# Sending attention scores through memory instead of through TensorE, in a two-layer graph network

## The chip, the cores and the metric

The kernel runs on one core of a Trainium2 chip. The metric is the device time of one execution in microseconds; several executions are timed and their median is taken. A profile of one execution gives, for each engine, when every instruction began and how long it took. The engines are TensorE (PE, with its weight loads shown as PEld), VectorE (DVE), ScalarE (ACT), GpSimd (POOL) and SyncE (SP), which here does nothing but issue DMAs.

## The reference, cut to what matters

There are 128 graphs of 64 nodes, each node a row of 768 numbers. Layer 0 mixes neighbours with three weight matrices and is not touched by the change, except in how it writes its last result to memory. Layer 1 is graph attention with 6 heads of 128 columns:

```python
h = jnp.einsum('bni,hio->bhno', feat_in, W)
th = jnp.tanh(h)
attn_src = jnp.einsum('bhno,hoz->bhnz', th, w_src)
attn_dst = jnp.einsum('bhno,hoz->bhnz', th, w_dst)
attn = attn_src + jnp.swapaxes(attn_dst, -1, -2)
attn = jnp.where(attn >= 0, attn, leaky_alpha * attn)
attn = jnp.where(mask, NEG_MASK, attn)
attn = jax.nn.softmax(attn, axis=-1)
feat_out = jnp.einsum('bhnm,bhmo->bhno', attn, h) + b
gate = jax.nn.sigmoid(feat_in @ H_w.T + H_b)
out = gate * feat_out + (1.0 - gate) * feat_in
```

So each node n has one source score and one destination score per head. The logit of the pair (n, m) is source score of n plus destination score of m. A node's own score lies on the partition of that node, and can be added there as a bias. The other node's score has to appear along the free axis, for all 64 nodes of the graph, on every partition: a turn and a spread. How that is done is what changes.

## The kernel before, in words

The 8192 rows are 64 tiles of 128 rows (two graphs each), worked on as 32 pairs of tiles. Pass 1 (layer 0) runs over all pairs, then pass 2 (layer 1) runs over all pairs. All five engines have an order of instructions written out by hand, SP too.

In pass 1, `finish` closes each pair: `dev` and `norm` make the layer norm of the result on ScalarE (`HF`), `turn` transposes its 32x32 blocks on VectorE into `HT` (L862), `put_turned` (called tput in the lists) stores `HT` to `H1D` in one DMA per tile (L865), and `half_of` makes `HH_` on ScalarE (L852). `HF`, `HT` and `HH_` share three buffers, so the second `HH_` of a pair waits until the first tile's `HT` has been stored. In pass 2, `load_h` reads `H1D` back as the operand of the products, with the blocks put into their right places by the read: four DMAs of 96 KB per tile, in pieces of 32 numbers (L372).

Pass 2 runs a list of step names, `ORDER`, once per pair. A name such as `cp1/2` means step `cp`, tile 1, of the pair that is two behind. `Pk.q` is a half product on TensorE: 30 per pair, each two 512-column instructions in the trace (L1121). `att` is the weighing of the rows (L1286). `R` and `RA` add products into `hz` on VectorE and ScalarE, `Ff` forms operands on VectorE. Each engine follows the list in its own instructions only, and runs ahead until something it needs isn't there. `END` is the list for the last pairs.

The path of the scores, tile by tile: `th` (tanh, ACT), `mul` (both products with the score weights, DVE, L1163), `sum` (sums by head, ACT, L1173), `k` and `chain` (POOL: separate the two graphs, L1176, and split the scores into three bf16 parts, L1184 and L1186), `rows` (PE, L1206: turn them), `rrow` (DVE, L1210) and `lrow` (ACT, L1215) take the result out of PSUM, `log` (PE, L1225: one product gives source plus destination for all heads), `cp` (DVE, L1229: take the logits where there is an edge, over a tile that `memset` filled), `pre` (ACT, L1234: leaky ReLU), `tr` (DVE, L1238: largest), `exp` (ACT, L1246). Then `tv` turns the blocks of the exponentials on DVE, `ts` stores them with four DMAs (L1272), `tl` loads them back (L1278), `swap` loads the other graph's rows (L1192), and `att` follows.

Pass 1 already has a small case of the form that the change brings to the scores: `turn_degrees` transposes a 128x32 tile on DVE (L603), `put_degrees` stores it (L606), and `get_degrees` reads it back with two loads that repeat a row over 64 partitions (L612).

Of the kernel before, what the change touches and what calls it, by code (L numbers as in the profile page):

```python
# [15 lines left out]
P = 128  # L16
# [81 lines left out]
dma0/4 R1/1 RA1/1 P3.1/1 R2/1 memset1/2 R14/2 th1/2 R3/1 tv1/3 P11.0/1 rows0/2 P4.0/1 rrow0/2  # L98
lrow0/2 tl0/3 mul1/2 P6.0/1 Ff1 P4.1/1 R4/1 Ff6/1 log0/2 P6.1/1 P11.1/1 sum1.2/2 R6/1 sum1.3/2
sum1.0/2 Ff7 sum1.1/2 P7.0/1 k1/2 cp0/2 Ff4 lx1/3 P7.1/1 rec0/3 Ff2 P9.0/1 Ff8 Ff11/1 R7/1 P9.1/1  # L100
pre0/2 RA7/1 tr0/2 chain1/2 P8.0/1 Ff9 P8.1/1 R9/1 lx0/3 rows1/2 Ff10 memset0/1 ld R11/1 g1/3
exp0.0/2 ts1/3 rrow1/2 R8/1 P10.0/1 P10.1/1 exp0.1/2 Ff3 swap0/3 lrow1/2 th0/1 P12.0/1 tv0/2 R10/1
P12.1/1 mul0/1 tl1/3 g0/2 att/3 log1/2 R12/1 ev1.0/3 ev1.1/3 cp1/2 sum0.3/1 ev0.0/3 sum0.1/1 P13.0/1
e1/3 f1.0/3 P13.1/1 P14.0/1 sum0.0/1 P14.1/1 P2.0 P2.1 R13/1 ev0.1/3 P1.0 pre1/2 f1.1/3 sum0.2/1
tr1/2 f1.2/3 P0.0 P0.1 e0/3 dma1/3 P5.0 f0.0/3 swap1/2 P5.1 exp1.0/2 RA0 R0 P1.1 exp1.1/2 f0.1/3
ts0/2 RA5 k0/1 chain0/1 rec1/2 Ff5 RA14/1 P3.0 f0.2/3 R5 RA2
# [4 lines left out]
FINISH = (158, 189, 215, 216, 242, 268)  # L111
# [4 lines left out]
P3.1/2 P11.0/2 RA1/2 Ff6/2 swap0/4 R2/2 R1/2 P4.0/2 R14/3 Ff1/1 rows0/3 Ff11/2 tv1/4 P4.1/2 Ff4/1  # L116
memset1/3 R3/2 rrow0/3 g0/3 tl0/4 th1/3 P8.0/2 lrow0/3 Ff2/1 P6.0/2 R4/2 P6.1/2 Ff3/1 log0/3 P7.0/2
P8.1/2 mul1/3 cp0/3 R6/2 pre0/3 sum1.2/3 ts1/4 Ff8/1 P7.1/2 Ff7/1 R7/2 tr0/3 rec0/4 RA7/2 Ff9/1
P9.0/2 P9.1/2 P11.1/2 tl1/4 Ff5/1 sum1.0/3 R9/2 R8/2 sum1.1/3 P10.0/2 R11/2 P10.1/2 sum1.3/3 th0/2
Ff6/1 Ff10/1 R10/2 att/4 P13.0/2 lx0/4 mul0/2 dma0/5 exp0.0/3 g1/3 ev1.0/4 g0/2 ev0.1/4 ev1.1/4  # L120
ev0.0/4 sum0.2/2 k1/3 g1/4 P13.1/2 P0.0/1 chain1/3 P12.0/2 P5.0/1 memset1/2 rows1/3 R13/2 rrow1/3
P2.0/1 e1/4 P1.0/1 e0/4 lx1/4 f1.0/4 f0.0/4 P12.1/2 f1.1/4 sum0.0/2 P2.1/1 lrow1/3 R12/2 ld/1 P5.1/1
log1/3 P0.1/1 f0.1/4 f1.2/4 exp0.1/3 sum0.3/2 P14.0/2 f0.2/4 R5/1 P14.1/2 sum0.1/2 RA0/1 P1.1/1 R0/1
P3.0/1 k0/2 cp1/3 RA2/1 R14/2 RA1/1 Ff11/1 R1/1 P3.1/1 RA14/2 tv0/3 pre1/3 chain0/2 tr1/3 lx0/3 R2/1
th1/2 rows0/2 mul1/2 P4.0/1 P8.0/1 lrow0/2 exp1.0/3 R3/1 rrow0/2 exp1.1/3 P8.1/1 tv1/3 P4.1/1 Ff1
sum1.2/2 memset0/2 lx1/3 R4/1 RA5/1 Ff2 Ff4 sum1.0/2 sum1.1/2 log0/2 Ff7 P6.0/1 P6.1/1 R6/1 Ff3
cp0/2 swap1/3 sum1.3/2 P7.0/1 k1/2 P7.1/1 P9.0/1 RA7/1 P9.1/1 R8/1 swap0/3 chain1/2 Ff8 pre0/2
rows1/2 ts0/3 P11.0/1 ts1/3 tr0/2 P11.1/1 tl1/3 lrow1/2 rec1/3 Ff9 exp0.0/2 rec0/3 R7/1 P10.0/1
exp0.1/2 rrow1/2 R9/1 Ff10 R11/1 dma0/4 log1/2 tv0/2 cp1/2 P10.1/1 R10/1 tl0/3 P12.0/1 P12.1/1 att/3
dma1/4 th0/1 pre1/2 P13.0/1 mul0/1 tr1/2 g0/1 R12/1 g1/2 sum0.0/1 sum0.1/1 P14.0/1 ev0.1/3 ev1.1/3  # L130
ev1.0/3 ev0.0/3 sum0.3/1 k0/1 sum0.2/1 e1/3 P13.1/1 e0/3 swap1/2 R13/1 f1.0/3 PH0 P14.1/1 swap0/2
f0.0/3 f1.1/3 RA14/1 PH2 exp1.0/2 R14/1 chain0/1 PH1 f1.2/3 PH5 exp1.1/2 RAH0 tv1/2 memset0/1 f0.1/3
rows0/1 f0.2/3 lrow0/1 th1/1 ts0/2 mul1/1 PH3 RAH5 PH11 RAH2 tl0/2 RAH1 PG0 RH3 PH4 Ff5 RH4 PH6 Ff6
dma0/3 sum1.0/1 PH7 sum1.2/1 rrow0/1 sum1.1/1 RH6 rec0/2 RAH7 log0/1 PH9 dma1/3 Ff11 lx0/2 cp0/1
sum1.3/1 k1/1 PH8 RG0 RH9 RH11 PH10 pre0/1 RH8 PH12 chain1/1 rows1/1 tr0/1 ts1/2 th0 RH10 lx1/2
rec1/2 tl1/2 mul0 memset1/1 rrow1/1 att/2 exp0.0/1 exp0.1/1 sum0.1 lrow1/1 PH13 PG3 tv0/1 ev0.1/2
RH13 ev0.0/2 log1/1 RH12 sum0.2 ev1.0/2 sum0.0 sum0.3 cp1/1 ev1.1/2 e0/2 pre1/1 lx0/1 PH14 swap0/1
f0.0/2 g1/1 ts0/1 tr1/1 PG2 RAH14 f0.1/2 RG2 k0 f0.2/2 chain0 e1/2 PG1 RG1 PG8 RG3 f1.0/2 PG4
exp1.0/1 PG5 exp1.1/1 dma0/2 rows0 th1 tv1/1 lrow0 swap0 RG4 f1.1/2 PG6 mul1 memset0 tl0/1 f1.2/2
sum1.1 RG6 rrow0 att0/1 rec0/1 PG7 PG9 log0 RG7 PG10 sum1.0 RG5 dma1/2 sum1.2 ev0.0/1 sum1.3 PG11  # L140
cp0 ts1/1 swap1/1 ev0.1/1 k1 pre0 tl1/1 RG9 chain1 tr0 e0/1 rows1 rec1/1 RG11 lrow1 f0.0/1 att1/1
exp0.0 lx0 rrow1 exp0.1 log1 f0.1/1 ev1.0/1 ev1.1/1 RG8 memset1 cp1 e1/1 turnp0 lx1/1 RG10 PG12 pT0
f1.0/1 rec0 pre1 f1.1/1 f1.2/1 att0 tr1 RG12 g0 PG14 exp1.0 ev0.0 PG13 ev0.1 e0.0 swap1 exp1.1 lx1
turnp1 dma1/1 f0.0.0 e0.1 f0.2/1 f0.1.0 f0.0.1 f0.2.0 RG13 f0.3.0 f0.1.1 rec1 out0.0 RG14 f0.2.1 pT1
att1 ev1.1 e1.1 ev1.0 g1 f1.0.1 dma0/1 e1.0 f0.3.1 f1.1.1 f1.0.0 out0.1 f1.2.1 f1.1.0 f1.3.1 f1.2.0
f1.3.0 out1.1 out1.0
# [4 lines left out]
def kernel(  # L151
# [82 lines left out]
    Q = 32  # L234
    NQ = P // Q


    H0D = [dram.tile([KB * P, P], F32, name=f"h0_{t}") for t in range(NT)]
    CTD = [dram.tile([4 * P, P], BF16, name=f"ct_{p}") for p in range(NP)]
# [127 lines left out]
    def load_h(p):  # L367
        for k in range(2):
            t = 2 * p + k
            H1[t] = keep.tile([P, D], F32, name="h1", tag="x", bufs=6)  # L370
            for f in range(NQ):
                nc.sync.dma_start(  # L372
                    H1[t][f * Q : (f + 1) * Q].rearrange("i (b n) -> i b n", n=Q),
                    H1D[p][k].rearrange("(b i) (f n) -> f i b n", i=Q, n=Q)[f])

    def fetch():


        def load_block(n):
            j, q = int(n[1]), int(n[2])  # L380
            to = bw2[n].rearrange("p (k s n) -> p k s n", k=KQ, s=2)
            for s, src in enumerate((w_cat, hw_t)):
                nc.sync.dma_start(
                    to[:, :, s, :],
                    src.rearrange("(j k p) n -> j p k n", k=KQ, p=P)[j][:, :, q * CQ : (q + 1) * CQ])

        return ([(62, lambda: load_h(0)), (67, lambda: nc.sync.dma_start(hbb, row(hb, P)))]
                + [(i, lambda n=n: load_block(n)) for i, n in (
                    (7, "b10"), (13, "b00"), (13, "b21"), (25, "b11"), (31, "b01"), (37, "b20"),
                    (49, "b22"), (49, "b02"), (61, "b12"))]  # L390
                + [(i, lambda n=n: sum_of_weights(bw2, n)) for i, n in (
                    (22, "g10"), (28, "g6"), (41, "g12"), (46, "u"), (50, "g14"), (57, "w"),
                    (59, "g5"), (65, "v"), (67, "g3"), (70, "g9"), (73, "g1"), (76, "g8"),
                    (79, "g11"))])


    with ExitStack() as px:
# [441 lines left out]
        def finish(p, k):  # L839
# [24 lines left out]
            def put_turned():  # L864
                nc.sync.dma_start(H1D[p][k].rearrange("(b p) n -> p b n", p=P),  # L865
                                  HT[t].rearrange("p (b n) -> p b n", b=KB))
# [174 lines left out]
    with ExitStack() as px:  # L1041
# [7 lines left out]
        def load(p):  # L1049
            if p >= NP:  # L1050
                return
            if p:
                load_h(p)
            AI[p] = work.tile([P, 2, N], I32, name="ai", bufs=4)
            nc.sync.dma_start(
                AI[p], adj[p * 2 * GT : (p + 1) * 2 * GT].rearrange("(t g) i j -> (g i) t j", g=GT))
# [22 lines left out]
        for g in range(GT):  # L1079
            nc.gpsimd.memset(gm[g * N : (g + 1) * N, g : g + 1], 1.0)  # L1080
        lrow, rrow, sdb = [], [], []
# [73 lines left out]
        TH, PR, SD, SG, PS, AM, AL, PB, DN, MX, PT, PO, FF, EE, HX, TP = ({} for _ in range(16))  # L1155
# [5 lines left out]
        def multiply(t):  # L1161
# [3 lines left out]
            SD[t] = small.tile([P, 2, H], F32, name="sd")  # L1165
            SG[t] = small.tile([P, 3, H], F32, name="sg")

        def sums(t, i):

            j = 1 - i // 2  # L1170
            for h in range(i % 2 * HH, (i % 2 + 1) * HH):
                to = SD[t][:, 1, h : h + 1] if j else SG[t][:, 2, h : h + 1]
                nc.scalar.activation(PR[t][:, j, h, :], PR[t][:, j, h, :], AF.Copy, accum_out=to)  # L1173

# [42 lines left out]
        def fill(t):  # L1217
            AM[t] = work.tile([P, H, N], F32, name="a")
            nc.gpsimd.memset(AM[t], NEG_MASK / LEAKY)
# [12 lines left out]
        def leaky(t):  # L1232
            al = AL[t] = work.tile([P, H, N], F32, name="al", bufs=1)
            nc.scalar.activation(al, AM[t], AF.Prelu, alpha=LEAKY)  # L1234
# [5 lines left out]
        def exps(t, i):  # L1240

            if i == 0:
                PB[t] = work.tile([P, H, N], F32, name="pb")
# [103 lines left out]
        def store(t):  # L1347
# [6 lines left out]
            "rec": one_over, "tv": turn_blocks, "ts": put_blocks, "tl": get_blocks, "turnp": turn_p, "pT": copy_p,  # L1354
# [5 lines left out]
        def step(n, p):  # L1360
            if n == "att":
                attend_both(p)
            elif n == "ld":
                load(p + 1)
            elif n[0] == "F":
# [158 lines left out]
```

## Time and profile before

| | |
|---|---|
| median of 3 runs | 2336.75 us (2336.64 to 2336.89) |
| profiled execution, its own time | 2335.71 us |
| its span | 2333.9 us |
| PE busy | 2308.5 us, 99% of the span |
| DVE busy | 1952.9 us, 84% |
| ACT busy | 1280.4 us, 55% |
| POOL busy | 442.2 us, 19% |
| mean granted TensorE clock | 0.997 |

The span is what the profiled engines cover; the execution's own time is 1.81 us longer. Pass 2 takes about the last 900 us of the span. Busy times in the profile add up overlapped instructions once, but the mean duration of one instruction includes the overlap with the next: the distance from one start to the next is what an engine really pays. In timelines the columns are start, duration, engine, line and operation.

### The profile page before, as it was taken

The numbers are of one execution on the slowest core, as the hardware profiler recorded it, in microseconds if no ns is written. First come the engines' busy times: TensorE is split into PE (matmuls) and PEld (weight loads), VectorE is DVE, ScalarE is ACT, GpSimd is POOL, SyncE is SP. The second block draws the span as 40 slices with busy tenths as digits, with TensorE's granted clock in tenths as the row PEclk, the third lists the DMA queues.
The fourth block names the chain that finished last, engine by engine and source line by source line (L and its number), as shares of the span: only waits on it lengthen the run. The fifth ranks groups of instructions, "written<-read, shape, count | busy, mean of one in ns | idle before, by whom it ended". The sixth has DMA issues, their size and how long they took to land.

```text
span 2333.9 us, 35510 instructions
## 1 busy us (share of the span) xinstructions
PE 2308.5 (99%) x11441; PEld 1645.1 (70%) x11441; DVE 1952.9 (84%) x3738; ACT 1280.4 (55%) x3843; POOL 442.2 (19%) x1097
## 2 busy tenths in 40 slices
PE   9999999999999999999999999999999999999996
PEld 7888888888888888888888885444444444444445
DVE  8877777777777777777777777899999999999999
ACT  3454454454454543543544523677776667776776
POOL 1111111111111111111111101122222222222222
PEclk9999999999999999999999999999999999999998
DMA  5335535535445446445445367667677777776667
GB/s 190 91 98 130 136 100 134 129 100 144 119 104 148 112 107 157 105 110 155 100 114 152 98 164 148 122 139 147 139 144 152 150 146 141 145 146 138 141 134 164
DMA packets 805127, 308.89 MB, mean 132 GB/s; under 512 B 622676, under 2 KB 755143, under 8 KB 804940
## 3 DMA queue, kind: packets, MB, share of 16 engines
q1 hardware_dynamic: 795868, 282.20, 50.6%
q0 software_dynamic: 8928, 24.38, 6.0%
q8 instruction: 90, 1.47, 0.3%
q14 instruction: 97, 0.79, 0.1%
q10 hardware_dynamic: 144, 0.04, 0.0%
HBM read 140.11 MB, written 140.87 MB: 120 GB/s over the span
## 4 chain that ended last, share of the span: by engine, by line
PE 95%; DVE 3%; DMA 2%; issue 0%; SPq 0%; ACT 0%; DVEq 0%; ACTq 0%
PE pwa L814 21%; PE pwb L814 18%; PE pwcd L814 14%; PE pma L1121 14%; PE pmb L1121 11%; PE pmd L1121 5%; PE pmc L1121 5%; PE pb L742 3%; PE ps L1286 1%; PE pwcd L798 1%; PE pwcd L742 1%; PE ps L1225 1%; DMA weights<-in_wself_t_dram 1%; DMA weights<-in_wadj_t_dram 1%; PE pmc L1286 0%
## 5 line engine op out<-in xcount | busy, mean ns | idle before, releaser
L814 PE MATMUL pwa<-weights,op 128*128 128x256 f32 x2304 | 529.6, 379 | 0.3 <-DVE x L806 0.3
L814 PEld LDWEIGHTS pwa<-weights,op 128*128 128x128 f32 x2304 | 427.5, 190 | 56.0 <-issue 1.1
L814 PE MATMUL pwb<-weights,op 128*128 128x256 f32 x1932 | 451.3, 381 | 0.0
L814 PEld LDWEIGHTS pwb<-weights,op 128*128 128x128 f32 x1932 | 361.9, 190 | 51.4 <-issue 0.8
L347 DVE TENSOR_TENSOR op<-op 128x768 f32<-128x768 f32 x310 | 290.2, 945 | 94.5 <-ACT op L752 91.6
L814 PE MATMUL pwcd<-weights,op 128*128 128x256 f32 x1560 | 357.8, 379 | 0.0
L814 PEld LDWEIGHTS pwcd<-weights,op 128*128 128x128 f32 x1560 | 296.1, 190 | 40.1
L1121 PE MATMUL pma<-weights,op_f 128*128 128x512 f32 x620 | 291.5, 592 | 0.0
L1173 ACT ACTIVATE pr<-pr 128x128 f32<-128x128 f32 x768 | 225.5, 295 | 89.0 <-DVE pr L1163 89.0
L752 ACT COPY op<-pb 128x512 f32<-128x512 f32 (+1 forms) x132 | 70.8, 617 | 357.0 <-PE pb L742 357.0
L1121 PEld LDWEIGHTS pma<-weights,op_f 128*128 128x128 f32 x620 | 117.7, 190 | 147.8 <-issue 138.4
L324 POOL TENSOR_SCALAR rn<-su 128x1 f32<-128x1 f32 x124 | 25.0, 202 | 846.8 <-ACT hf L319 528.5
L1121 PE MATMUL pmb<-weights,op_f 128*128 128x512 f32 x372 | 181.0, 594 | 0.0
L547 ACT ACTIVATE hp<-x,rn 128x768 f32<-128x768 f32 x60 | 109.2, 1820 | 108.6 <-POOL rn L326 108.6
L1173 ACT ACTIVATION_READ_ACCUMULATOR pr<-pr 128x1 f32 x768 | 143.5, 187 | 0.0
L318 ACT ACTIVATE hf<-x 128x768 f32<-128x768 f32 x64 | 53.6, 837 | 148.9 <-DVE x L850 148.8
L1246 ACT ACTIVATE pb<-al,mx 128x64 f32<-128x64 f32 x384 | 128.1, 337 | 12.6 <-DVE mx L1238 12.4
L1348 POOL DMA_DIRECT2D out_dram<-f x62 | 55.1, 898 | 390.4 <-DVE f L1345 372.0
L1121 PEld LDWEIGHTS pmb<-weights,op_f 128*128 128x128 f32 x372 | 68.4, 190 | 84.0 <-issue 76.3
L1121 PE MATMUL pmb<-weights,h 128*128 128x512 f32 x248 | 122.8, 596 | 0.0
L806 DVE TENSOR_TENSOR x<-pwcd,x 128x256 f32<-128x256 f32 x127 | 53.3, 420 | 81.7 <-PE pwcd L798 81.5
L1121 PE MATMUL pmc<-weights,op_f 128*128 128x512 f32 x248 | 121.6, 592 | 0.0
(240 smaller groups left out, 4121.0 us busy)
## 6 DMA issues: line engine op xcount, KB each, us to landing
x<-in_x_dram SPq DMA_DIRECT2D x64, 384.0 KB
h<-ht SPq DMA_DIRECT2D x64, 384.0 KB
out_dram<-x SPq DMA_DIRECT2D x64, 384.0 KB
hh<-hh SPq DMA_DIRECT2D x64, 384.0 KB
h<-h SPq DMA_DIRECT2D x256, 96.0 KB
x<-hh SPq DMA_DIRECT2D x64, 384.0 KB
out_dram<-f POOLq DMA_DIRECT2D x62, 384.0 KB, 6.2
h<-hpt SPq DMA_DIRECT2D x60, 384.0 KB
```

The costliest lines, as they stand in the source:

```text
L318: nc.scalar.activation(by, src, AF.Copy, scale=-1.0 / D, accum_out=sums[:, 0:1])
L324: nc.gpsimd.tensor_scalar(to[:, 0:1], sums[:, 1:2], 1.0 / D, EPS, op0=OP.mult, op1=OP.add)
L347: return (nc.vector.tensor_add if s1 == "+" else nc.vector.tensor_sub)(to, x, y)
L547: nc.scalar.activation(hp.rearrange("p (b f i) -> p b f i", b=KB, f=NQ), X[t].rearrange("p (b i f) -> p b f i", b=KB, f=NQ), AF.Relu, scal ...
L742: nc.tensor.matmul(to[:, g, :, i, :], H0[2 * p + k][o, kb * P : (kb + 1) * P], rts[p % 2][o, k, :n].rearrange("p s n -> p (s n)"), start=T ...
L752: nc.scalar.copy(a[:, :n].rearrange("p s h (g n) -> p g (s h) n", g=GT), ps[:, :, c * n * KQ * N : (c + 1) * n * KQ * N].rearrange("p g (x ...
L806: nc.vector.tensor_add(v, bank[b][:, :CQ], v)
L814: nc.tensor.matmul(bank[b][:, :CQ], OPS[p, an][:, s, q, :], bw[bn][:, (s * KQ + q) * CQ : (s * KQ + q + 1) * CQ], start=(first and q == s ...
L1121: nc.tensor.matmul(bank[p, b], operand(p, an)[:, q, :], bw2[bn][:, 2 * q * CQ : 2 * (q + 1) * CQ], start=(first and q == 0), stop=(q == KQ ...
L1173: nc.scalar.activation(PR[t][:, j, h, :], PR[t][:, j, h, :], AF.Copy, accum_out=to)
L1246: nc.scalar.activation(PB[t][:, h, :], AL[t][:, h, :], AF.Exp, bias=MX[t][:, h : h + 1], accum_out=DN[t][:, h : h + 1])
L1348: nc.gpsimd.dma_start(of[t * P : (t + 1) * P, :], FF[t], accum_op=OP.add)
```

## The change

For all pairs but the last two (`BY_PE = 2`), the two products on TensorE and what serves them (`k`, `chain`, `rows`, `rrow`, `lrow`, `log`, `pre`) are gone. The sums of the destination scores go into a 128x32 tile `sdt`, which VectorE transposes (`sv`); one DMA stores it to memory (`ss`), two DMAs read it back with every head's 64 scores repeated over the 64 partitions of the graph (`sl`); ScalarE then does, for each head, the leaky ReLU of that plus the source score as a bias (`lk`), and VectorE chooses by edge from SBUF (`cl`). The other edit moves the reordering of `H1D`: `put_turned` now stores with four DMAs in pieces of 32 numbers, and `load_h` reads each tile with one DMA. `le` loads the second tile of a pair at its own place. `ORDER`, `END` and `FINISH` are new lists.

```diff
+    BY_PE = 2
+    SDD = [dram.tile([P, Q], F32, name=f"sd_{t}") for t in range(NT)]
...
-    def load_h(p):
-        for k in range(2):
+    def load_h(p, *ks):
+        for k in ks:
             t = 2 * p + k
             H1[t] = keep.tile([P, D], F32, name="h1", tag="x", bufs=6)
-            for f in range(NQ):
-                nc.sync.dma_start(
-                    H1[t][f * Q : (f + 1) * Q].rearrange("i (b n) -> i b n", n=Q),
-                    H1D[p][k].rearrange("(b i) (f n) -> f i b n", i=Q, n=Q)[f])
+            nc.sync.dma_start(H1[t].rearrange("p (b n) -> p b n", b=KB),
+                              H1D[p][k].rearrange("(b p) n -> p b n", p=P))
...
             def put_turned():
-                nc.sync.dma_start(H1D[p][k].rearrange("(b p) n -> p b n", p=P),
-                                  HT[t].rearrange("p (b n) -> p b n", b=KB))
+                for f in range(NQ):
+                    nc.sync.dma_start(
+                        H1D[p][k].rearrange("(b i) (f n) -> f i b n", i=Q, n=Q)[f],
+                        HT[t][f * Q : (f + 1) * Q].rearrange("i (b n) -> i b n", n=Q))
...
-            SD[t] = small.tile([P, 2, H], F32, name="sd")
+            SD[t] = sdt[t % 2] if t // 2 < NP - BY_PE else small.tile([P, 2, H], F32, name="sd")
...
+        def turn_scores(t):
+            ST[t] = work.tile([P, Q], F32, name="st2")
+            nc.vector.transpose(ST[t], SD[t])
+
+        def put_scores(t):
+            nc.sync.dma_start(SDD[t], ST[t])
+
+        def get_scores(t):
+            DR[t] = work.tile([P, GT, H, Q], F32, name="dr")
+            for g in range(GT):
+                at = SDD[t][g * N : g * N + H, :]
+                nc.sync.dma_start(
+                    DR[t][g * N : (g + 1) * N].rearrange("p f h n -> p f (h n)"),
+                    bass.AP(tensor=at.tensor, offset=at.offset,
+                            ap=[[0, N], [Q * Q, N // Q], [1, H * Q]]))
+
+        def leaky_sum(t):
+            PB[t] = work.tile([P, H, N], F32, name="pb")
+            for h in range(H):
+                nc.scalar.activation(PB[t][:, h, :].rearrange("p (f n) -> p f n", n=Q),
+                                     DR[t][:, :, h, :], AF.Prelu, alpha=LEAKY,
+                                     bias=SG[t][:, 2, h : h + 1])
+
+        def choose_leaky(t):
+            AL[t] = AM[t]
+            nc.vector.copy_predicated(AM[t], AI[t // 2][:, t % 2, None, :].to_broadcast([P, H, N]),
+                                      PB[t])
...
-            nc.gpsimd.memset(AM[t], NEG_MASK / LEAKY)
+            nc.gpsimd.memset(AM[t], NEG_MASK if t // 2 < NP - BY_PE else NEG_MASK / LEAKY)
...
-            al = AL[t] = work.tile([P, H, N], F32, name="al", bufs=1)
+            al = AL[t] = work.tile([P, H, N], F32, name="al", tag="dr")
```

Where the new steps stand in the new `ORDER` (steps between them left out, P steps kept where they measure the distance):

```
lk0/3 ... cl0/3 ... tr0/3 sv1/3 ... ss1/3 ... sl1/3 ... att/4 ... sv0/2 ... lk1/3 le/1 ... cl1/3 ss0/2
... swap1/3 P5.1/1 ts0/3 sl0/2 R1/1 P3.0/1 lx1/3 ... swap0/3 P3.1/1 ... P4.0/1 ... tl0/3 ... ts1/3
```

## The prediction

> **What bounds the kernel now.** I read the page's engine totals and chain, then the busy time by stretches, then the PE timeline of one pair.
>
> The page's first and fourth part:
>
> ```profile
> PE 2308.5 (99%) x11441; PEld 1645.1 (70%) x11441; DVE 1952.9 (84%) x3738; ACT 1280.4 (55%) x3843; POOL 442.2 (19%) x1097
> PE 95%; DVE 3%; DMA 2%; issue 0%; SPq 0%; ACT 0%; DVEq 0%; ACTq 0%
> ```
>
> TensorE is never without work and is 95% of the chain. That is an average over two passes, so the stretches come next (columns: length, then busy us and count of PE, PEld, DVE, ACT, POOL, then clock, DMA share, GB/s):
>
> ```profile
> 1100.00:1200.00 100.00, 100.00 (x582) 86.95 (x581) 72.89 (x134) 46.43 (x76) 15.27 (x44) 1.00 0.51 130
> 1850.00:1950.00 100.00, 100.00 (x421) 46.26 (x420) 96.87 (x202) 70.19 (x311) 25.99 (x57) 1.00 0.69 144
> 2300.00:2334.00 34.00, 19.20 (x167) 13.85 (x166) 30.55 (x72) 16.39 (x63) 5.21 (x12) 0.82 0.70 163
> ```
>
> In the middle of pass 2, PE is busy 100 of 100 us at full clock. VectorE has 3.1 us of 100 free, ScalarE 30, the DMA engines 31%. So a PE instruction that goes is a gain only if VectorE keeps up. PE idles only at the end: 14.8 of the last 34 us, with 3.2 more in the 50 us before (46.80 of 50).
>
> What PE pays, from starts in its timeline:
>
> ```profile
> 1654.37 1.88 PE L1121 MATMUL pma<-weights,op_f 128*128 128x512 f32 x4
> 1656.18 0.32 PE L1286 MATMUL ps<-weights,pT 64*64 64x128 f32 x1
> ...
> 1657.65 0.34 PE L1225 MATMUL ps<-rrow,lrow 82*128 82x384 bf16 x1
> 1657.83 1.88 PE L1121 MATMUL pmb<-weights,h 128*128 128x512 f32 x4
> 1659.54 1.88 PE L1121 MATMUL pma<-weights,op_f 128*128 128x512 f32 x4
> ...
> 1670.70 0.25 PE L1206 MATMUL ps<-idr,sdb 128*82 128x192 bf16 x1
> 1670.79 1.05 PE L1121 MATMUL pmb<-weights,h 128*128 128x512 f32 x2
> 1671.67 1.02 PE L1121 MATMUL pma<-weights,h 128*128 128x512 f32 x2
> 1685.54 0.34 PE L1225 MATMUL ps<-rrow,lrow 82*128 82x384 bf16 x1
> ```
>
> Four L1121 start 1.72 us before the next four, so one costs 0.429 us, not its duration. The same L1225 returns after 27.89 us: that is one pair. Sixty L1121 are 25.75 us. The attention stretch runs from the end of the fourth product (1654.37 + 1.72 = 1656.09) to L1225 at 1657.65, 1.56 us. Together 27.31; what is left, 0.57 us per pair, is the two L1206 and two L1225. Directly: L1225 at 1657.65, next start 1657.83, 0.17 to 0.18; L1206 takes 0.09 and makes the next two products last 0.88 instead of 0.86, about 0.115. Twice 0.29 is 0.57 again. The durations (0.246 and 0.331) would say 1.15 per pair, which is twice too much because of the overlap.
>
> **The change part by part.** Durations from the groups view (columns: busy us, mean ns, idle before):
>
> ```profile
> L1246 ACT ACTIVATE pb<-al,mx 128x64 f32<-128x64 f32 x384 | 128.1, 337 | 12.6 <-DVE mx L1238 12.4
> L1229 DVE COPY_PREDICATED a<-ai,ps 128x384 f32<-128x384 int32 x64 | 36.8, 574 | 0.1
> L1210 DVE TENSOR_TENSOR rrow<-ps,de 64x384 bf16<-64x384 f32 x64 | 34.0, 531 | 3.0
> L603 DVE STREAM_TRANSPOSE dt<-dgs 128x32 f32<-128x32 f32 x30 | 6.3, 212 | 1.0
> ```
>
> *PE.* 60 of 64 `rows` and `log` go (the last four tiles keep them): 30 pairs by 0.57 = 17.1 us off the path.
>
> *VectorE.* Per tile `rrow` goes (531 ns) and a 128x32 transpose comes (212, the same shape as in pass 1): 0.64 us less per pair. Busy is 96.87% of 27.88 = 27.01 us now, and 26.37 after, against a PE pair of 27.31: 0.94 us free where 0.87 is free now. The choice now reads SBUF instead of PSUM; no row shows that. The reduce of the same 384 elements from SBUF takes 538 and the choice from PSUM 574, so I keep 574; at 450 or 700 the pair moves by 0.25 us either way, inside the 0.94. If that cover were gone, each 0.1 us per pair would cost 3 us.
>
> *ScalarE.* Per tile `lrow` (L1215, mean 257 in the same view) and `pre` (L1234, 509) go and six Prelu of 128x64 come. Nearest row is the exponential of that shape, 337, so 2.02 us: per pair 4.04 - 1.53 = 2.5 us more, on 70.2% of 27.88 = 19.6. That is 22.1 of 27.3, 81%. Prelu already stands between Copy and Exp without a gap, so I add no table change. Cost 0 while ScalarE has 5 us free; the lower end, 250 ns from start to start, makes it 1.5 instead of 2.5.
>
> *POOL.* Six instructions per tile go: 464 + 3 x 279 + 2 x 507 = 2.3 us. POOL is at 26%, so 0.
>
> *The new wait.* `sl` waits on SP for the store of `ss` to land, and `lk` waits on ScalarE for `sl`. Pass 1 has the same form (store L606, loads L612), and pass 2 another (L1272, L1278). SP's own waits (sum, times, longest):
>
> ```profile
> SPq L612 <- DMA rd<-dt: 40.7, 30, 1.7
> SPq L1278 <- DMA pt<-tp: 52.3, 66, 2.7
> SPq L1192 <- PE ps L1286: 179.2, 29, 10.7
> ```
>
> So SP stands 1.4 to 1.7 us behind such a store, at most 2.7. Two loads take about 1.1 us to issue; their landing has no row, and I take 2.5 us (SP waited for the store that L572 reads for 2.6 us in the mean: 76.7 over 30). From `ss` to data in place is then some 6 us. By the new list, with 0.858 us for a half product: `sl1` stands at 8.6 us and `lk1` at 17.0; `sl0` at 24.7 and `lk0` at 29.9 (2.6 in the next turn). The first has 8.4 us for issue and landing (3.6) plus up to 2 of waiting; the second 5.2, and its store was issued 6 us earlier. SP can run ahead too: of 27.9 us it now stands 6.2 at L1192, waiting for attention to free a buffer, and the new list puts `swap` after attention. Behind a waiting `sl1` are only the `load_h` DMAs, first used in the next turn. Behind a waiting `sl0` are `lx1`, `swap0`, `tl0` and `ts1`, and `tl0` feeds attention 12.9 us later. Cost 0; ends: 0 and the rival below.
>
> *SP and DMA in pass 2.* Per pair six DMAs come for scores, and `load_h` shrinks from eight in 128-byte pieces to two: the same 25 issues. Eight L372 hold SP for 8.3 us in the pair from 1664. A gain for SP, worth nothing on the path, since the operands are loaded a turn ahead.
>
> *The stores in pass 1.* Per tile four DMAs for one: six more issues per pair, some 0.5 us each, ahead of `load_own` (L572) and `getct` (L710). The four L1272 stores of 192 KB end their issue at 1661.17 and the load behind them goes at 1662.73, landed in under 1.6 us; twice the bytes I take at 3.2. So `hh` of the second tile, which needs this buffer, waits not 1.9 but about 1.9 + 1.5 + 1.6 = 5.0 us. What hides it:
>
> ```profile
> 705.62 0.93 ACT L852 ACTIVATE hh<-hf,half 128x768 f32<-128x768 f32 x1 [1.87 <-DMA h<-ht]
> 718.22 2.05 ACT L752 COPY op<-pb 128x512 f32<-128x512 f32 x4 [11.67 <-PE pb L742]
> ```
>
> ScalarE has nothing for 11.67 us behind it. L856 on SP, which stores `hh`, goes at 710.04; `hh` would end at 709.7. `load_own` is 2 us later, its operands being used from 719. Cost 0. A rule speaks against this edit: the Trainium skill, "DMA: Bandwidth & Descriptors", Specifications, says that below 512 B a transfer is a read-modify-write and misses line rate, and now the small pieces are written, not read. By rows: queue 1 spent 50.6% of 16 engines' 2333.9 us on 795,868 packets, 23.7 ns each in the mean over all sizes, so a tile's 3072 packets are at most 4.6 us. By the rule I double it (an estimate): 9.1 us per tile, 18.3 of a 43 us pair, share 0.51 to about 0.9, and `hh` waits some 10 us, just within the cover. By the row the sum is 0; by the rule it is still 0, but with nothing spare. I take the row, because the L1272 stores are small writes too and land in 1.6 us; the rule widens the high end by 5 us.
>
> *The ends.* The last two pairs keep the old path, and `END` is rewritten, around 18 us of PE idle. I take 0, with 3 us either way.
>
> The sum: 2335.71 (profiled execution, 1.81 over its span) - 17.1 = 2318.6. The median is 1.04 above the profiled run, so 2319.6.
>
> **The rivals.**
>
> *Part of it is given back.* VectorE goes from 96.9% of the old period to 96.6% of the new one. For: every wait there over 0.94 us per pair becomes PE time, and `cl` now follows a ScalarE step that is 1.3 us longer than the old one. Against: before, at the same fill, PE lost nothing. At 0.25 us per pair lost, 30 x 0.25 = 7.5 us: 2327.
>
> *Slower: VectorE stands at `cl0` for the scores.* Mechanism: SP issues `sl0` only after `swap1` and four `ts0` stores; if its data come late, ScalarE stops at `lk0` and VectorE, in order, at `cl0`, with everything for PE's operands behind. It decides from a stall of 0.94 us per pair on; at 0.94 + 0.57 = 1.5 us the whole gain is gone. With one more DMA latency (2.5 us) the loss is 1.56 x 30 = 47 us: 2366. Against: the 5.2 us between, and SP's slack.
>
> *It doesn't do what it says.* The products go, but PE's period stays at 27.88 because VectorE or ScalarE sets it: 2336. Against: the tallies 26.4 and 22.1.
>
> **How the numbers follow.** No change is anything within 0.2%, 4.7 us, about what measurement of this kernel can tell. Full gain 0.66 (2314 to 2323), part given back 0.22 (2323 to 2332), no change 0.04, slower 0.08. Faster is the first two, 0.88. The likeliest is 2319.6. The range starts at 2314 (a tail 3 us better, 2 more for the overlap at the removed products) and goes to 2329, most of the second case, leaving out about 0.17 above and 0.03 below.
>
> **What would show it.** Right: the PE timeline has products back to back with one pair every 27.3 us, PE 100 of 100 in mid pass 2, DVE near 96.5%, ACT near 80%; SP waiting 1.4 to 2.7 us for the score store; `hh` in pass 1 waiting about 5 us, and pass 1 no longer than before. Wrong: PE gaps at L1121 or L1286 released by VectorE, VectorE idle before the choice, released by ScalarE and that by the `dr` loads; or a pass 1 with PE waiting for `op`.

## The result and the profile after

The changed kernel takes 2325.34 us in the median of 5 runs (2324.63 to 2325.83). The kernel before took 2336.64 in the same comparison (2336.4 to 2336.89). The ratio is 0.9951, with a 95% interval of 0.9937 to 0.9966: faster by 11.3 us, where 17.1 was forecast (2319.6, range 2314 to 2329).

The page's totals and chain, changed kernel:

```profile
PE 2296.6 (99%) x11321; PEld 1638.9 (71%) x11321; DVE 1934.8 (83%) x3738; ACT 1319.2 (57%) x4083; POOL 309.7 (13%) x739
PE 94%; DVE 3%; DMA 2%; issue 0%; SPq 0%; ACT 0%; DVEq 0%; ACTq 0%
```

The same three stretches as before (length, then busy us and count of PE, PEld, DVE, ACT, POOL, then clock, DMA share, GB/s):

```profile
1100.00:1200.00 100.00, 100.00 (x582) 86.96 (x581) 72.88 (x134) 46.38 (x76) 15.25 (x44) 1.00 0.58 131
1850.00:1950.00 100.00, 100.00 (x367) 45.76 (x366) 96.28 (x202) 76.44 (x353) 9.87 (x15) 1.00 0.71 167
2300.00:2334.00 34.00, 10.39 (x90) 6.95 (x89) 20.50 (x50) 11.48 (x36) 1.77 (x2) 0.80 0.43 101
```

The changed kernel's span ends at 2324.1, so its last stretch holds only 24.1 us. TensorE has 120 instructions fewer and is still without a gap in the middle of pass 2. VectorE is at 96.3%, ScalarE went from 70 to 76, POOL from 26 to 10. In pass 1 only the DMA share has changed, from 0.51 to 0.58.

TensorE's timeline around one attention (attention's own 64x64 products, which begin at 1762.29, are cut out):

```profile
1758.76 1.88 PE L1134 MATMUL pmb<-weights,op_f 128*128 128x512 f32 x4
1760.48 1.88 PE L1134 MATMUL pma<-weights,op_f 128*128 128x512 f32 x4
...
1763.76 1.98 PE L1134 MATMUL pmb<-weights,h 128*128 128x512 f32 x4
1765.58 1.88 PE L1134 MATMUL pma<-weights,op_f 128*128 128x512 f32 x4
1767.30 1.88 PE L1134 MATMUL pmd<-weights,h 128*128 128x512 f32 x4
```

Four products start 1.72 us before the next four everywhere (1765.58 to 1767.30), except straight behind attention: there it is 1.82 (1763.76 to 1765.58), and the duration shown is 1.98 instead of 1.88. Attention begins at 1734.87, 1762.29 and 1789.71, so a pair takes 27.42 us. It was 27.88, and 27.31 was forecast.

The weight loads (PEld) show where the 0.10 lies. Behind attention, changed kernel first, kernel before second:

```profile
1763.76 0.30 PEld L1134 LDWEIGHTS pmb<-weights,h 128*128 128x128 f32 x2 [0.17 <-DVE weights L1163]
```

```profile
1657.65 0.10 PEld L1225 LDWEIGHTS <-lrow 82*128 82x128 bf16 x1 [0.17 <-issue]
1657.65 0.36 PEld L1121 LDWEIGHTS pmb<-weights,h 128*128 128x128 f32 x2
```

Elsewhere the weights of a large product begin to load with the product ahead of it, 0.43 us before they are needed. Behind attention's 64x64 products they begin only with the product itself, at 1763.76, and that product lasts 0.70 instead of 0.59. In the kernel before they began at 1657.65, under the logit product, 0.17 us before theirs at 1657.83, and that product lasted 0.59.

The new and the changed instructions in the groups view (busy us, mean ns | idle before):

```profile
L1213 ACT ACTIVATE pb<-dr,sg 128x64 f32<-128x64 f32 x360 | 91.7, 333 | 1.4 <-DMA dr<-sd 1.4
L858 ACT ACTIVATE hh<-hf,half 128x768 f32<-128x768 f32 x64 | 59.9, 936 | 98.0 <-DMA h<-ht 96.9
L1219 DVE COPY_PREDICATED a<-ai,pb 128x384 f32<-128x384 int32 x60 | 34.9, 581 | 0.7 <-ACT pb L1213 0.7
L1193 DVE STREAM_TRANSPOSE st<-sdt 128x32 f32<-128x32 f32 x60 | 12.0, 200 | 1.4 <-ACT pr L1187 1.4
```

The scores have to be waited for almost never: the first Prelu of a tile (L1213) stood 1.4 us in all for its loads, the choice (L1219) 0.7 us in all for Prelu. SP's own waits, in total, times and longest:

```profile
SPq L1196 <- DVE st L1193: 119.9, 32, 10.0
SPq L1204 <- DMA sd<-st: 53.9, 31, 2.9
```

SP waits for the store of the scores (L1204) 1.7 us in the mean and 2.9 at most.

Where the profiled executions part: early in pass 2 a product of layer 1 begins at 1424.76 in both. The first attention begins 0.95 us earlier than before, the 26th 12.37 us earlier (2185.93 and 2173.56): 25 pairs by 0.457 between them. The spans end 9.8 us apart. So pass 1 gave and took nothing, the pairs gave 0.46 each, and in these two executions the end took something back:

```profile
2185.93:2333.90 147.97, 130.07 (x693) 71.94 (x692) 141.78 (x307) 103.39 (x456) 37.08 (x81) 0.96 0.68 145
```

is that end before, and after it is

```profile
2173.56:2324.10 150.54, 129.90 (x680) 71.66 (x679) 140.74 (x307) 108.31 (x486) 21.77 (x46) 0.95 0.68 157
```

TensorE and VectorE are busy no longer, and the stretch takes 2.57 us more. Most of that is chance, for the end varies by 1.8 us from one profiled execution to the next: counted from the 26th attention, it takes 149.7 us in the profiles of e1 and e5 below, which have the old `END`, and 150.86 and 149.08 in those of e2 and e12, which have the new one. The middle ones of each three, 149.7 and 150.5, are 0.8 us apart.

### The profile page after: what moved, and what is told of

Read it like the earlier page. It is cut to its first block, busy times and chain, and to the rows that moved or that the text cites. A ratio compares the mean times of both kernels' runs of the same rounds, so it can differ in the third digit from the quotient of the medians.

```text
span 2324.1 us, 35384 instructions
## 1 busy us (share of the span) xinstructions
PE 2296.6 (99%) x11321; PEld 1638.9 (71%) x11321; DVE 1934.8 (83%) x3738; ACT 1319.2 (57%) x4083; POOL 309.7 (13%) x739
## 3 DMA queue, kind: packets, MB, share of 16 engines
q8 instruction: 89, 1.46, 0.3%
## 4 chain that ended last, share of the span: by engine, by line
PE 94%; DVE 3%; DMA 2%; issue 0%; SPq 0%; ACT 0%; DVEq 0%; ACTq 0%
PE pwa L820 20%; PE pwb L820 17%; PE pwcd L820 14%; PE pma L1134 14%; PE pmb L1134 12%; PE pmd L1134 5%; PE pmc L1134 5%; PE pb L748 3%; PE ps L1334 1%; PE pwcd L804 1%; PE pwcd L748 1%; DVE weights L355 1%; DMA weights<-in_wself_t_dram 1%; DMA weights<-in_wadj_t_dram 0%; PE pmc L1334 0%; DVE f L1371 0%
## 5 line engine op out<-in xcount | busy, mean ns | idle before, releaser
L1134 PE MATMUL pma<-weights,op_f 128*128 128x512 f32 x620 | 297.0, 593 | 0.1
L1134 PE MATMUL pmb<-weights,op_f 128*128 128x512 f32 x372 | 175.1, 592 | 0.0
L1294 ACT ACTIVATE pb<-a,mx 128x64 f32<-128x64 f32 x360 | 119.6, 335 | 2.2 <-DVE mx L1285 2.1
L680 DVE TENSOR_REDUCE sum<-eq 128x26 f32<-128x1664 bf16 x64 | 120.0, 1875 | 0.1
```

Source lines behind the costliest of these rows:

```text
L680: nc.vector.tensor_reduce(SUM[p][:, k], EQ[p, k], AX.X, OP.add)
L1134: nc.tensor.matmul(bank[p, b], operand(p, an)[:, q, :], bw2[bn][:, 2 * q * CQ : 2 * (q + 1) * CQ], start=(first and q == 0), stop=(q == KQ ...
L1294: nc.scalar.activation(PB[t][:, h, :], AL[t][:, h, :], AF.Exp, bias=MX[t][:, h : h + 1], accum_out=DN[t][:, h : h + 1])
```

## The experiments

Times are medians; ratios are to the kernel before, measured beside each. In most of these kernels the lists stand on fewer lines, so a step's line number is lower than in the changed kernel; what it is can be read from the names.

**e1: the logit product away from attention.** In the kernel before, `log1` and `cp1` move from straight behind attention to behind the next half product.

```diff
-att/3 log1/2 R12/1 ev1.0/3 ev1.1/3 cp1/2 sum0.3/1 ev0.0/3 sum0.1/1 P13.0/1
+att/3 R12/1 ev1.0/3 ev1.1/3 sum0.3/1 ev0.0/3 sum0.1/1 P13.0/1 log1/2 cp1/2
```

> The kernel before, with the logit product of tile 1 and its choice moved in ORDER from right behind attention to behind the next half product, so that an f32 product follows attention directly. Theory T (the first f32 product behind attention takes 0.10 us longer, and the logit product hid that): a pair goes from 27.88 to 27.98 us, 30 pairs cost 3 us, about 2339.7. Rival (the 0.10 us per pair in the changed kernel comes from its new order or its memory traffic): the pair stays at 27.88, 2336.7.

Measured: 2339.08 against 2336.77, ratio 1.0011 (1.0003 to 1.0019), and 27.976 us per pair instead of 27.882. TensorE's timeline behind attention:

```profile
1770.13 1.12 PE L1083 MATMUL pmb<-weights,h 128*128 128x512 f32 x2
1771.09 0.33 PE L1187 MATMUL ps<-rrow,lrow 82*128 82x384 bf16 x1
1771.26 1.02 PE L1083 MATMUL pmb<-weights,h 128*128 128x512 f32 x2
```

The two products behind attention now last 1.12 and occupy 0.96 instead of 1.02 and 0.86. The logit product costs its 0.17 where it stands now, and the 0.10 has appeared behind attention, where the weights again begin to load with their product, at 1770.13. So it is no property of the new operations: the first large product behind attention costs 0.10 more, and the logit product had covered that. The profile of before shows it too, in its `END`, at an attention that no logit product follows:

```profile
2241.34 1.98 PE L1121 MATMUL pmb<-weights,h 128*128 128x512 f32 x4
2243.16 1.88 PE L1121 MATMUL pma<-weights,op_f 128*128 128x512 f32 x4
```

1.98 and 1.82 again. The removed product therefore gave 0.07 net at that place, not 0.17.

**e2: can a small product cover it?** The changed kernel with one bf16 product of 8 columns where the logit product stood.

```diff
             if first and q == 0:
                 bank[p, b] = psm.tile([P, 512], F32, name=f"pm{b}", bufs=2 if b == "a" else 1)
+                if k == 13 and p + 2 < NP:
+                    nc.tensor.matmul(bank[p, b][:, :8], idr[:, N:], idr[:, :8], start=True, stop=True,
```

> The changed kernel, with one bf16 product of 8 columns added behind attention in every pair but the last two, into the bank that the next product starts over (its result is not used). Theory T: the bf16 product takes over the place of the logit product, the f32 product behind it starts clean, and the pair goes from 27.42 to between 27.35 (0.03 for the small product) and 27.42: 2323.3 to 2325.3. Rival (the 0.10 us has another cause): it only adds its own 0.03 to 0.1 us, 27.45 to 27.52, 2326 to 2328.

Measured: 2325.94, ratio 0.9956 (0.9943 to 0.9968), 27.42 us per pair. But product 13 isn't the first of its bank, so the condition is never true and nothing was added; TensorE has 11321 instructions as in the changed kernel. The run tells nothing of the question. It is a second measurement of the changed kernel, 0.6 us from the first.

**e12: the same, with the product issued.**

```diff
+            if k == 13 and q == 0 and 1 < p < NP - 2:
+                nc.tensor.matmul(bank[p, b][:, :8], idr[:, N:], zero,
+                                 start=False, stop=False, skip_group_check=True)
```

> The changed kernel, with one bf16 product of 8 columns (of zeros, added to the bank that the next product uses) straight behind attention in 28 pairs. In the run called e2 that product stood behind a condition that is never true and was not issued (the profile counts 11321 instructions on TensorE in both kernels), so e2 only repeats the changed kernel; this is the same question asked again, with the product in the list of instructions. Theory T: the first 128x128 product behind the 64x64 products of attention costs 0.10 us extra whatever it follows that is of that form, and a small bf16 product in between takes it: the next four products are 1.72 apart again instead of 1.82, and the pair goes from 27.42 to between 27.33 and 27.43 us, depending on what the small product costs itself (0.01 to 0.10); whole time 2322.5 to 2325.5. Rival R: the product does not take it, the four stay 1.82 apart, or the 0.10 falls on the small product instead and comes on top: 27.44 to 27.54, whole time 2325.5 to 2328.5.

Measured: 2325.54, ratio 0.9952 (0.9938 to 0.9965), 27.44 us per pair. Behind attention:

```profile
1764.48 0.18 PE L1135 MATMUL pmb<-zero,idr 128*128 128x8 bf16 x1
1764.52 1.96 PE L1139 MATMUL pmb<-weights,h 128*128 128x512 f32 x4
1766.32 1.88 PE L1139 MATMUL pma<-weights,op_f 128*128 128x512 f32 x4
```

```profile
1764.48 0.31 PEld L1139 LDWEIGHTS pmb<-weights,h 128*128 128x128 f32 x2
```

The small product occupies 0.04, and the four behind it are 1.80 apart: it takes 0.02 of the 0.10 and costs more than it takes. The pair is 0.02 longer, the rival's lower edge. The weights of the next product now begin to load 0.04 us ahead of it. So a lead of 0 costs 0.10 (e1 and the changed kernel), one of 0.04 costs 0.08 and one of 0.17, under the logit product, costs nothing: the 0.10 is the part of a weight load that nothing covers. Why the load starts no earlier behind the 64x64 products, no run here shows.

**e5: only the reordering of h1.** The kernel before, with `put_turned` and `load_h` of the changed kernel.

```diff
-            for f in range(NQ):
-                nc.sync.dma_start(
-                    H1[t][f * Q : (f + 1) * Q].rearrange("i (b n) -> i b n", n=Q),
-                    H1D[p][k].rearrange("(b i) (f n) -> f i b n", i=Q, n=Q)[f])
+            nc.sync.dma_start(H1[t].rearrange("p (b n) -> p b n", b=KB),
+                              H1D[p][k].rearrange("(b p) n -> p b n", p=P))
...
-                nc.sync.dma_start(H1D[p][k].rearrange("(b p) n -> p b n", p=P),
-                                  HT[t].rearrange("p (b n) -> p b n", b=KB))
+                for f in range(NQ):
+                    nc.sync.dma_start(
+                        H1D[p][k].rearrange("(b i) (f n) -> f i b n", i=Q, n=Q)[f],
+                        HT[t][f * Q : (f + 1) * Q].rearrange("i (b n) -> i b n", n=Q))
```

> The kernel before, with only the reordering of h1 moved from the loads of pass 2 to the stores of pass 1; scores and lists as before. Theory (both passes have the cover: ScalarE's 11.7 us gap in pass 1, operands loaded a turn ahead in pass 2): no change, within 1 us of 2336.7, both periods as before. Rival (the small written pieces hold up pass 1): 0.1 us or more per pair, from 2340 on.

Measured: 2337.45 against 2336.64, ratio 1.0005 (0.9997 to 1.0013): no change. Its stretches:

```profile
700.00:1000.00 300.00, 300.00 (x1669) 261.20 (x1668) 227.12 (x411) 142.97 (x224) 47.95 (x126) 1.00 0.54 124
1850.00:1950.00 100.00, 100.00 (x421) 46.20 (x421) 96.87 (x202) 70.46 (x311) 25.98 (x57) 1.00 0.60 146
```

Pass 1 costs TensorE nothing; its DMA share goes from 0.48 to 0.54 (both over 700 to 1000), and that of pass 2 falls from 0.69 to 0.60. By itself this is worth nothing.

**e6: only the scores.** The changed kernel with the stores and loads of h1 as they were, the opposite of the diff above.

> The changed kernel, with h1 stored and loaded as before (eight small-piece loads per pair in pass 2, some 8 us of SP's time, between the score loads of tile 1 and the score store of tile 0). Theory: SP reaches the score store of tile 0 about 2 us later, the scores still land before ScalarE asks, so 27.42 us per pair stays: 2325 to 2327. Rival (the reorder was needed to make room on SP): a stall of 0.3 us or more per pair, from 2334 on.

Measured: 2330.8, ratio 0.9975 (0.9967 to 0.9982), 5.5 us more than the changed kernel. A stretch, and ScalarE's waits between 1500 and 2100:

```profile
1850.00:1950.00 100.00, 100.00 (x367) 45.76 (x366) 96.29 (x201) 76.30 (x350) 9.87 (x15) 1.00 0.83 169
```

```profile
ACT pb L1213 <- DMA dr<-sd: 17.5, 13, 3.5
```

The DMA share is 0.83 instead of 0.71, and Prelu now waits for its scores 13 times. Most pairs still take 27.42, but two took 29.02 and 29.05, and the first pair of `END` 31.72 instead of 29.25: 1.6 + 1.6 + 2.5 = 5.7 us, about the difference. Neither number expected came, but the mechanism is seen in SP's waits between 1500 and 2100, changed kernel first:

```profile
SPq L1196 <- DVE st L1193: 83.9, 23, 4.5
SPq L1204 <- DMA sd<-st: 39.4, 22, 2.3
```

```profile
SPq L1204 <- DMA sd<-st: 39.6, 22, 2.2
```

In the changed kernel SP arrives at the store of the scores (L1196) early and stands 3.6 us for VectorE's turn. In e6 this wait is gone, and the wait for the store to land is as it was. So the eight loads use up the time that SP had to spare, and the scores come too late now and then. The store lands no slower; whether the loads of the scores, behind more small pieces on the same queue, do was not separated. The single runs of e6 lie between 2328.4 and 2336.5. The reordering is worth nothing alone and 5.5 us beside the scores.

**e7: the new operations in the old order.** The changed kernel with `ORDER`, `END` and `FINISH` of before and the names exchanged in place.

```diff
-k1/2 ... chain1/2 ... log1/2 cp1/2 ... rows, rrow, lrow, pre
+sv1/2 ... ss1/2 sl1/2 ... lk1/2 cl1/2
```

> All operations of the change, in the lists of before: transposing at the place of the separation, store and loads at the place of the split, leaky sum at the place of the logit product, choice where it was. Theory L (without new lists SP, waiting for the scores, holds up the stores and loads that feed attention): two to four us more per pair than 27.42, 2385 to 2445. Rival (the operations alone bring the gain): 27.4 to 27.5 per pair, 2325 to 2329.

Measured: 2707.21, ratio 1.1587 (1.1572 to 1.1603), 40 to 41 us per pair in the middle of pass 2. A stretch, and the waits between 1500 and 2100:

```profile
1700.00:1800.00 100.00, 79.53 (x285) 37.94 (x286) 63.22 (x136) 50.28 (x231) 6.01 (x9) 0.86 0.48 105
```

```profile
ACT pb L1169 <- DMA dr<-sd: 73.8, 15, 5.3
DVE st L1149 <- ACT pr L1143: 72.6, 14, 5.5
```

`k` and `chain` stood on POOL, which had time to wait for the sums of ScalarE. `sv` stands on VectorE: at the same place in the list it stops VectorE for 5.2 us each time, SP behind it, and ScalarE waits 4.9 us for the loads. The direction was as expected and the size far off, some 13 us per pair more than in the changed kernel: each wait stops an engine that executes in order, with all that stands behind it there. The granted clock is 0.86 in this stretch, so TensorE's products are slower too; how much of the 13 us that makes was not separated. So the new lists are part of the change and not beside it; without them the kernel is 370 us slower than before.

**e8: the loads of the scores late.** The changed kernel with one name moved in `ORDER`.

```diff
-ts0/3 sl0/2 R1/1 ... tl0/3 th1/2 R5/1 ts1/3
+ts0/3 R1/1 ... tl0/3 th1/2 R5/1 ts1/3 sl0/2
```

> The changed kernel, with the score loads of tile 0 moved in SP's order from behind the exponentials' store of tile 0 to the end of the list, behind that of tile 1: some 4.5 us later. Theory (VectorE, in order, stands at the choice until ScalarE has the scores, and only about 1 us per pair is free): 2 to 3.5 us more per pair, 2385 to 2430. Rival (the engines run ahead enough to take it): 27.4 to 27.5 per pair, 2325 to 2329.

Measured: 2498.04, ratio 1.0691 (1.0677 to 1.0706), 34.0 us per pair. The waits between 1500 and 2100, and one of them in VectorE's timeline:

```profile
ACT pb L1169 <- DMA dr<-sd: 117.1, 18, 7.3
DVE a L1175 <- ACT pb L1169: 90.1, 18, 5.8
```

```profile
1717.26 0.58 DVE L1175 COPY_PREDICATED a<-ai,pb 128x384 f32<-128x384 int32 x1 [4.96 <-ACT pb L1169]
```

This is the slower rival of the prediction in full: the loads late, ScalarE at `lk0`, VectorE at `cl0`, TensorE behind it. One misplaced name turns 11 us of gain into 161 of loss. A pair loses 6.6 us, more than was expected, and about what ScalarE now waits once in each (117.1 over 18 is 6.5).

**e9: how much time does VectorE have left?** The changed kernel with four transposes of 128x128, whose result nobody uses, ahead of each choice.

```diff
+            for _ in range(4):
+                nc.vector.transpose(scr, wsd[:, 0, :P])
```

> The changed kernel, with four extra 128x128 transposes on VectorE ahead of each choice, their result unused: some 1.8 us more of VectorE per pair (0.22 us each from start to start). Theory (VectorE is next in line: it has 3.85% of 27.42, 1.06 us, free per pair, and only what is over that becomes TensorE time): about 0.75 us more per pair, 22 us, near 2347. Rival (VectorE's free time is not usable, all of it is lost): 1.8 per pair, near 2378. Rival (VectorE has cover elsewhere): no change, 2325.

Measured: 2373.36, ratio 1.0152 (1.0139 to 1.0166), 29.02 us per pair.

```profile
1750.00:1850.00 100.00, 96.39 (x398) 42.88 (x398) 98.27 (x222) 72.19 (x326) 9.00 (x14) 1.00 0.66 153
```

The transposes in VectorE's timeline, with the choice behind them:

```profile
1758.39 1.34 DVE L1177 STREAM_TRANSPOSE scr<-wsd 128x128 f32<-128x128 f32 x4
1759.65 0.55 DVE L1178 COPY_PREDICATED a<-ai,pb 128x384 f32<-128x384 int32 x1
```

Four of them take 1.26 us from their start to the start of the choice, 0.32 each where 0.22 was expected, so 2.5 us of work came per pair and not 1.8. The pair is 1.60 longer, so 0.9 us was taken up without loss, of the 1.02 that VectorE had free (3.72% of 27.42). VectorE is busy 98.27%, and between 1500 and 2100 the profile lists no wait of VectorE, while TensorE waits for its results: VectorE sets the pair now. The theory held, with a wrong size for the transposes: 2.53 - 1.02 = 1.5 us. Work over the free time becomes TensorE time, and nearly all of the free time was cover, for work put at these two places.

**e3, e4, e10, e11: the end.** Four edits of `END` look for what it gives back. In the changed kernel TensorE has one gap of 3.2 us there:

```profile
2278.09 1.03 PE L1437 MATMUL pma<-weights,op_f 128*128 128x256 f32 x4
2282.29 2.04 PE L1437 MATMUL pmc<-weights,op_f 128*128 128x256 f32 x4 [3.17 <-DVE f L1371]
2284.13 1.53 PE L1437 MATMUL pmb<-weights,h 128*128 128x256 f32 x4
2285.49 1.03 PE L1437 MATMUL pma<-weights,op_f 128*128 128x256 f32 x4
```

and VectorE, between 2199 and the end, two waits that before did not have:

```profile
DVE f L1371 <- DMA out_dram<-f: 1.5, 1, 1.5
DVE f L1371 <- PE ps L1334: 1.1, 2, 0.9
```

e3 frees the bank that the gap waits for sooner:

```diff
-ev1.1/2 log1/1 cp1/1 ... PH12 ev1.0/2 PG5
+ev1.1/2 ev1.0/2 log1/1 cp1/1 ... PH12 PG5
```

> The changed kernel, with one division step in END (ev1.0 of the second last pair) moved forward to its sister, so that TensorE's bank is free before the choice and the largest of the next tile. Theory A (the 3.2 us TensorE gap before the first product into that bank, and the half clock that follows it, are what the end lost): the gap goes, 2 to 4 us faster, about 2322. Theory B (the end is VectorE's, and a TensorE gap there costs nothing): within 0.7 us of 2325.3.

Measured: 2327.34, ratio 0.9961 (0.9948 to 0.9975). This is no faster than the changed kernel, where 2 to 4 us faster was expected. The gap fell from 3.2 to under 1 us, and another came (TensorE's waits in `END`):

```profile
PE pmb L1393 <- DVE weights L1408: 5.1, 1, 5.1
```

e4 gives one more tile its own output buffer, so that VectorE needn't wait for the store:

```diff
-... if t == NT - 2 else
+... if t in (NT - 2, NT - 4) else
```

> The changed kernel, with the result tile of the second last pair's first tile put into a spare buffer, so that VectorE does not wait there for a store to land. Theory B (the end is VectorE's, and its 1.5 us wait for the store is part of what the end lost): about 1.5 us faster, 2323.8. Theory A (TensorE's gap decides): no change, 2325.3.

Measured: 2326.28, ratio 0.9955 (0.9942 to 0.9967). No gain came, where 1.5 us was expected. The wait of 1.5 us is gone, and the one for attention, which waits for a load of rows, has grown (VectorE's waits, then TensorE's):

```profile
DVE f L1327 <- PE ps L1290: 2.5, 3, 1.3
```

```profile
PE ps L1290 <- DMA hx<-weights: 1.6, 2, 1.3
```

e10 moves the last score steps of the new kind forward (`sl1/2`, `lk1/2`, `cl1/2`, `tr1/2`, `exp1.0/2`, `exp1.1/2`, `tv1/2`, `ts1/2`), e11 is e10 and e4 together:

```diff
-P14.1/2 ... sl1/2 ev0.1/3 f1.0/3 lk1/2 ts0/2 cl1/2 ... tr1/2
+ss1/2 sl1/2 tv0/2 ... mul0/1 lk1/2 ... cl1/2 sum0.3/1 PH0 R12/1 tr1/2
```

> The changed kernel, with the last tile that goes through memory moved forward in END: its score loads, leaky sum, choice, largest, exponentials, turn and store stand several steps earlier. Theory C (the end lost time because the last tile through memory reaches attention late, with VectorE idle around it): attention of that pair begins 2 to 4 us earlier and the end is 1 to 3 us shorter, 2322.5 to 2324.5. Rival (the end has so many tight waits that the gap only moves, as with the two edits of END before): within 1 us of 2325.5.

> The same as the run before it, with the spare result buffer of the earlier experiment as well. Theory C: 0.5 to 1.5 us below the run before it. Rival (the gap only moves): the same as it within 0.7 us.

Measured: 2326.6, ratio 0.9953 (0.9941 to 0.9966), and 2327.5, ratio 0.9954 (0.9941 to 0.9968). The gains expected did not come. TensorE's gap of 3.2 us stands as it was, and the attention that was to begin 2 to 4 us earlier begins 1.3 us later in e10, counted from the 26th (2277.18 - 2174.04 against 2275.39 - 2173.56). The intervals of all four overlap that of the changed kernel. VectorE is busy 115.8 of the last 124.8 us, and where a named wait was taken away another took its place. So none of the four edits found a single step that costs the end its time; what does stays open.

One part of it was not the list. In the profile of the changed kernel the granted clock (third number from the right) falls to 0.50 after that gap; in e12, with the same `END` and a gap of 3.25 us at the same place, it stays at 1.00. The three microseconds from 2282, changed kernel first, e12 second:

```profile
2282.00:2285.00 3.00, 2.71 (x7) 2.20 (x8) 3.00 (x4) 3.00 (x13) 0.00 (x0) 0.50 0.91 241
```

```profile
2282.00:2285.00 3.00, 2.62 (x12) 2.36 (x13) 3.00 (x4) 3.00 (x13) 0.00 (x0) 1.00 0.88 234
```

The end of e12 is 1.46 us shorter. But e2 spends twice as long at half clock as the changed kernel (6.8 us, 3.4 there) and its end is only 0.3 longer, so the clock is not all of it either.

## Why the prediction was right, and where a size was off

*The term that was mis-sized: TensorE, 30 pairs by 0.57.* Measured is 0.46, so 13.8 us instead of 17.1. The prediction took the cost of a product as the distance from its start to the next start. For the two `rows` and the other logit product that held, as far as the 0.46 that is left tells. For the one behind attention it did not: the 0.17 us there ran beside a delay of 0.10 that comes whether it stands there or not. The delay is a weight load that starts too late; it was taken as nothing. e1 shows this without any of the new operations (+0.094 per pair when the same product is only moved), e12 and the weight loads show what the time goes to, and the last attention stretches of before had it in view. This is 3.3 of the 5.8 us that are missing.

*The ends: 0, with 3 us either way.* By the medians they took 2.5 us (13.8 - 11.3), which the margin holds. About 1.8 of it is what four pairs that still ran in the end should have given there; the other 0.7 is less than the end varies between executions. In the two profiled executions the ends took about 4.4 (12.4, and 1.8 for the pairs to come, against 9.8), since the one before was 1.04 us under its median and the one after 0.49 over. Which step of the new `END` costs this stays open. A sure answer would need the old `END` with the new operations, which e7 could not give because its pass 2 was disturbed far earlier.

*VectorE: 26.37 us of a pair.* Measured 26.40, with the choice from SBUF at 581 ns (574 taken) and the transpose at 200 (212). That step held, and so did its reading: of the "0.94 us free" that was called cover, e9 used 0.9 before TensorE lost anything.

*ScalarE and POOL.* Six Prelu follow each other at about 0.25 us, the lower end named; 76.4% instead of 81. POOL cost nothing.

*The new wait.* 1.7 us in the mean, 2.9 at most, where 1.4 to 1.7 and 2.7 were read from two rows of the same form. That the loads arrive in time was right, but it hangs on the lists: e8 shows that the place of one name decides it, and e6 that it also needs the shorter `load_h`. "Worth nothing on the path" was right for the reordering alone (e5) and wrong beside the scores, where 5.5 us hang on it.

*Pass 1's stores.* The longest wait of the second `HH_` is 4.7 us, 5.0 were worked out, in the mean 3.2 (before 2.0), and ScalarE's idle time hid it: PE 300 of 300 before and after. The Trainium skill, "DMA: Bandwidth & Descriptors", Specifications, was taken as a doubling of the cost of the small pieces, which would have brought the share of pass 1 to 0.9; the share went from 0.48 to 0.54, that is 2.6 us in a pair of 43 us, or 1.3 us for the four stores of a tile with 3072 pieces in place of one with 768. What the page says, that pieces under 512 B miss the full rate, is seen here: between 700 and 1000 of the changed kernel a packet of 128 B took 13.4 ns in the mean and one of 512 B 28.0, so the same bytes cost 1.9 times as much. Too high was what the prediction made of it: the 23.7 ns per packet that it doubled is a mean over all sizes, and the large store that goes was not taken off. The 3072 pieces cost 2.6 us of 16 engines, not 4.6 or 9.1, and the 768 that they replace cost 1.3.

*The rivals.* "Part is given back" put the time at 2327, close to what came, but by VectorE's waits becoming TensorE time, and TensorE has none in the middle of pass 2; that the result lies near it is chance. "Slower" is real as a mechanism (e8) and was avoided by the list, with the shorter `load_h` beside it (e6). "It doesn't do what it says" is excluded by 27.42.

## What to carry to other kernels

The worth of an instruction that goes is the distance between its neighbours' starts with it and without it, so look for a place in the profile where the same neighbours meet without it (here the last attentions) before multiplying by the number of pairs. Look at the weight loads too: a product that goes may have been the cover of the next one's load. When work moves from an engine with time to spare to an engine or queue near its limit, its place in that engine's order decides more than its duration: with the new operations at the old places the kernel is 370 us slower, though the transpose itself takes 0.2 us. Before adding up what an engine near its limit can still take, read the cost of the added work from start to start: here 0.32 us and not 0.22 turned a loss of 0.75 us per pair into one of 1.60.

## What was not expected of the hardware

- The first four 128x128 products behind attention's 64x64 products are 1.82 us apart instead of 1.72, because the first one's weights begin to load with it and not 0.43 us ahead. A product of 384 columns in between hides this whole, one of 8 columns hides 0.02 of it.
- A gap of 3.17 us on TensorE was followed by slow products: four took 2.04 and the next four 1.53 us instead of 1.03, and from start to start 1.84 and 1.36 instead of 0.87, so the gap costs TensorE 1.5 us more than its length. The granted clock was 0.50 meanwhile. The Trainium skill, "TensorE: Matmul & The Clock Gate", Part 1, gives about 3.4 us of idle time as what halves the clock; here a little less was enough, and in e12 a gap of 3.25 us was not (granted clock 1.00, products of 1.10 and 1.03), so the length of a gap alone does not decide.
- Writes of 128 bytes were hardly dearer in DMA time than reads of 128 bytes: with the reordering moved from loads to stores, pass 1's share rose by 0.06 of a 43 us pair, 2.6 us, and pass 2's fell by 0.09 of a 27.9 us pair, 2.5 us (e5).
